# Two graph-attention layers on one core: V's products among the first scores, layer 0's sums by VectorE

## The chip, the core and the metric

The kernel runs on one core of a Trainium2 chip. A core has a matrix engine (TensorE, PE in the profile; its loads of the stationary operand are listed apart as PEld), a vector engine (VectorE, DVE), a scalar engine (ScalarE, ACT), a general one (GpSimd, POOL), and a queue that issues most DMA transfers (SyncE, SP). Each engine takes its instructions strictly in the order written and waits on semaphores for what others have to finish. Matmul results go to PSUM, which this kernel uses as four single banks of 512 columns and two pairs of banks; everything else is in SBUF. The metric is the time of the kernel on the device in microseconds; lower is better.

## What is computed

64 graphs of 256 nodes with 512 features, all in float32. Two layers, one after the other:

```python
# layer 0: one attention over the graph, scores of rank one
feat_proj = einsum('bnh,oh->bno', feats, fc_w) + fc_b
logits = q + swapaxes(k, 2, 1)             # q, k: one number per node
masked = logits + (1.0 - adj_mat) * NEG_INF
masked = where(masked >= 0, masked, 0.01 * masked)
x = einsum('bnm,bmh->bnh', softmax(masked), feat_proj) + feats
# layer 1: eight heads of 64
Q, K, V = x @ W_q + b_q, x @ W_k + b_k, x @ W_v + b_v      # by heads
scores = Q K^T / 8 + a[:, :, None] + c[:, None, :] + b_g + log(adj + 1e-9)
x = softmax(scores) V + x
```

## The kernel before, in words

Two graphs make a group: 512 nodes, 32 groups. Layer 0's weights e0 are kept transposed (neighbours on partitions). The features are mixed first (`mix`, tile `y`) and projected after, so that the projection and the three products of layer 1 are all of the form 512x512 by 512x512. Each of these is done in a Strassen-like way, with seven block products instead of eight: `pf` (layer 0's projection), `pq`, `pk`, `pv`. Their steps are called `p1` to `p7`; each is four matmul instructions of 256 columns, which stand as eight records in the trace (float32 takes two passes). `p1` starts an accumulation in a bank, `p6`, `p5` and `p3` add to it, and between them ACT copies its state out (`keep`); `p7` and `p4` share a second bank, `p2` has its own. VectorE forms the sums (`sum_00`, `sum_11`, `sum_10`; `sum_01` for `pf`) and, before the products, the sums of the moving operand's blocks (`ysum:0..3` in tile `tb`, `xsum:0..3` in tile `t1b`). p6 needs the second of these, p7 the third, p4 the fourth.

The loop is a software pipeline written out by hand (`step`, L1041, and `attention_and_layer_0`, L1000). One step works on four groups: D finishes its output, A is in layer 1's attention, F in layer 0's last part and in layer 1's products, and X, the next, is loaded and gets its layer-0 weights. The strings in these functions are lists of methods, called in that order; with `tc.manual_schedule` each engine's instructions stand in just that order.

One step's order on PE, before: scores 0 of A; `totals_1` of D (two small matmuls with `every`, which sum layer 1's weights over a graph and spread the sums over the partitions); `sums` of F (layer 0's sums as a product with a column of ones, L594); scores 1; V's `p3`, `p4` of A; `mix:0`, `mix:1`; a transpose of the layer-0 sums (`rc`, L604); `mix:2`, `mix:3`; `pf`'s p1, p2, p6, p7, p5; scores 2; `attend:0` (weights times V for graph 0 of A, tile `oT`); `totals_0`; scores 3; `pf` p3; Q's p1; `pf` p4; `attend:1`; K's p1; then Q's, K's and V's other products.

The names that matter:

- `scores:u` (L801) fills a pair of banks for each of the two neighbour tiles; ACT takes the exponent (L815), VectorE multiplies by the adjacency (`factor`, L821), and `both` adds the two tiles (L828). `parts:u` transposes that sum in 32x32 blocks and adds up its blocks' rows (L857, L858); `totals` finishes it on PE.
- `turn`, `divide`, `complete`, `store` make the output from `oTs`, the copy of `attend`'s result: a transpose (L923), a product with the reciprocal sums (L943), the residual's addition (L951) and four DMA issues on SP (L981).
- `send:o:k` transposes one block of x1 on VectorE (L729) and writes it to DRAM on SP (L733); `fetch` reads it back as four DMAs (L747), `fetch_by_both` on SP and ACT by halves. `copy:n` (L376) makes a contiguous copy of one block of x1 for V's products.
- `adjt` transposes the adjacency (L545) and makes the mask, (a - 1) * 1e9, on VectorE (L546); `add_eps` is on ACT (L550); `weights` forms e0 (L579, L583) and its exponent (L584). `dot_q`, `dot_k`, `keys` are dot products along rows on VectorE (L509); `spread` sends the result through DRAM to all partitions.
- `residual:gr` adds V's bias to x1 on ACT (L772), `turn_residual:gr` transposes it (L786).

`Mixed.keep` (L488) adds on GpSimd; that is all its work inside the loop. e0's sums, before: eight matmuls with four column positions of the array, a copy by ACT, a transpose on PE, a reciprocal on VectorE.

Of the kernel before, what the change touches and what calls it, by code (L numbers as in the profile page):

```python
# [25 lines left out]
def kernel(  # L26
# [96 lines left out]
    eps = const.tile([P, 1], F32, tag="eps", name="eps")  # L123
    nc.gpsimd.memset(eps, 1e-9)

    def column(src, tag, pool=const, q=nc.sync):
# [35 lines left out]
    def fast():  # L162
        main = ExitStack()
        with main:
# [49 lines left out]

            every = const.tile([P, HD], F32, tag="every", name="every")
            for q in range(P // B):
                for n in range(HD // B):
                    rows = slice(q * B, (q + 1) * B)
                    nc.gpsimd.tensor_copy(every[rows, ts(n, B)], ident[rows, rows])
# [167 lines left out]
            class Product:  # L387
# [3 lines left out]


                def __init__(self, name, a, b, out, rows, bias=None):
                    self.name, self.a, self.b, self.out = name, a, b, out
                    self.rows, self.bias = rows, bias
# [17 lines left out]

                def fresh(self, n):
                    dst = bank(f"{self.name}_{n}").rearrange("p (m k) -> p m k", m=2)
                    self.add(n, dst, True)
                    return dst
# [36 lines left out]
                def p7(self):  # L454
                    self.r2 = self.fresh(7)

# [49 lines left out]
            def dot_rows(src, w_row, init, dst, name):  # L506
# [5 lines left out]
                )  # L512

            class Group:

# [57 lines left out]
                def weights(self, jc):  # L573
# [10 lines left out]
                    nc.scalar.activation(e, e, AF.Exp)  # L584

                def sums(self):

                    sm = sm0.pop("bank", None)
                    begun = sm is not None
                    sm = (sm if begun else bank(f"sm0_{self.g}"))[:, 0:P]  # L590
                    for jc in range(TPG):
                        for t in range(T):
                            gr, ic = divmod(t, TPG)
                            nc.tensor.matmul(  # L594
                                sm[ts(t, RS), :], lhsT=ones[:, 0, :], rhs=self.e0[:, jc, gr, ts(ic, P)],
                                start=(jc == 0 and not begun), stop=(jc == TPG - 1),
                                tile_position=(0, t * RS), skip_group_check=True,
                            )
# [3 lines left out]
                def recip(self):  # L602
                    pt = bank(f"rc_{self.g}")[:, 0:P]
                    nc.tensor.transpose(pt, self.sms, ident)  # L604
# [29 lines left out]
                def features_first(self):  # L634

                    g = self.g
                    xT = one.tile([P, NC, TOK], F32, tag="qT", name=f"xT_{g}")
                    fp = one.tile([P, T, D], F32, tag="v", name=f"fp_{g}")
                    for t in range(T):
# [24 lines left out]
                    for t in range(T):  # L664
                        self.dot_k(t)
                    self.adjt()
                    product(1)
# [11 lines left out]
                    add_constants()  # L679
                    self.recip()  # L680
                    self.begin()
# [20 lines left out]
                def begin(self):  # L702

                    g = self.g

                    def to(dst):
                        return lambda o, k: block(dst, o, k)

                    def to_v(o, k):
                        return self.v[:, TPG * k : TPG * (k + 1), o * HALF : (o + 1) * HALF]  # L710


                    self.d = {}
# [4 lines left out]
                    self.v = one.tile([P, T, D], F32, tag="v", name=f"v_{g}")  # L718
                    b, c, self.xsum, self.copy = blocks_of_x1(self.x1T, f"t1b_{g}")
                    self.pv = Product(f"pv_{g}", "v", c, to_v, True)  # L720
                    self.pq = Product(f"pq_{g}", "q", b, to(self.qT), False, bq_col)
                    self.pk = Product(f"pk_{g}", "k", b, to(self.kT), False)

# [139 lines left out]
                def totals(self, gr, dst):  # L863
# [3 lines left out]
                    for par in range(2):  # L867
                        nc.tensor.matmul(  # L868
                            dst[par * HD : (par + 1) * HD, :].rearrange("p (a m) -> p a m", a=2),
                            lhsT=every, rhs=self.part[:, :, par * half : (par + 1) * half],  # L870
                            start=True, stop=True, skip_group_check=True,
# [3 lines left out]
                def totals_1(self):  # L875

                    sm0["bank"] = bank(f"tot_{self.g}_1")
                    self.totals(1, sm0["bank"][:, P : P + NC * N // B])

# [120 lines left out]
            def attention_and_layer_0(D, A, F, X, check):  # L1000

                A("pv.sum_11 scores:0")
                D("totals_1")
                F("sums")
                A("scores:1 pv.p3 pv.p4 factor:0:0 factor:0:1")
                D("ratios:1")
                A("both:0 factor:1:0 pv.sum_10 factor:1:1 both:1")
                check()
                F("mix:0 mix:1 ysum:0 recip")
                D("divide:1")  # L1010
                A("parts:0 residual:1")
# [12 lines left out]
                F("pk.p1 pk.keep_1")  # L1024

# [12 lines left out]

            checked, sm0 = {}, {}

            def step(d, a, f, n, check):  # L1041
# [19 lines left out]
                else:  # L1061
                    f.features_first()
                    F("pq.p1 pq.keep_1 pk.p1 pk.keep_1")
# [275 lines left out]
```

## Time and profile before

| | us |
|---|---|
| median of three runs | 2344.75 (2343.78 to 2345.67) |
| the profiled execution's own time | 2344.13 |
| its span in the profile | 2342.3 |
| ScalarE's share of the span | 42% |
| GpSimd's share | 6% |
| L801 `sc` matmuls, 2048 records, busy | 255.7 |
| L841 `oT` matmuls, 2032 records, busy | 233.4 |
| L594 `tot<-e,ones` matmuls, 480 records, busy | 19.3 |
| L604 `rc<-ident,sms` transposes, 32 records, busy | 8.7 |
| VectorE's longest wait in total: L821 for ACT's exponent | 49.6 |

All times in the profile come from one execution: its span of 2342.3 lies within its own time of 2344.13, which is 0.62 below the median of the three timed runs. The TensorE clock granted in it was 0.998 of the full one. In the groups a row reads: line, engine, operation, tile written <- tiles read, partitions x elements, count, busy time and mean duration of one. A matmul's end is modelled; its start is not. Since 16 records that follow each other overlap in the profile, the time that a group takes of PE is read from its start to the next group's start. A line of the timeline gives start and duration from the span's begin, engine, line and tiles, and in brackets the idle time before it and what ended it.

The DMA issues of one step on SP, in order: the adjacency (four), D's output (four), the four `send`s and `fetch`es of x1, the next x (one transfer of 1024 KB, which lands 5.2 us after its issue in the median, 5.0 to 8.1), A's output for graph 0 (four), and two for `spread`.

### The profile page before, as it was taken

What the parts mean: (1) busy time and instruction counts of PE and PEld (TensorE: products, weight loads), DVE (VectorE), ACT (ScalarE), POOL (GpSimd) and SP (SyncE); (2) the same over time, 40 slices, a digit from 0 to 9 for tenths busy, and PEclk for the clock granted to TensorE, in tenths of its full rate; (3) what the DMA queues carried; (4) which work ended last, traced back from release to release, by engine and by line L of the source; (5) the groups of instructions that cost most, each with busy time, mean ns of one, the idle gap of its engine ahead of it and who ended that gap; (6) DMA issues with size and microseconds to landing.
All of it is one profiled execution on the core that took longest, in us unless ns stands there. A gap on an engine that the chain in (4) does not pass through costs nothing.

```text
span 2342.3 us, 34561 instructions
## 1 busy us (share of the span) xinstructions
PE 2324.0 (99%) x13203; PEld 1907.7 (81%) x13203; DVE 2083.5 (89%) x3026; ACT 980.7 (42%) x1710; POOL 130.4 (6%) x111
## 2 busy tenths in 40 slices
PE   9999999999999999999999999999999999999997
PEld 5888888888888888888888888888888888888885
DVE  6798989889889989999899889998998989999897
ACT  3444344444444344444434444434444344444443
POOL 0000000000000000000000000000000000000000
PEclk9999999999999999999999999999999999999999
DMA  4122332223322233322233232332223332223312
GB/s 131 46 59 73 77 82 59 63 64 86 77 73 55 59 81 77 77 61 59 71 78 81 61 64 61 86 77 72 58 61 77 78 79 62 56 71 81 77 50 38
DMA packets 517267, 163.90 MB, mean 70 GB/s; under 512 B 415188, under 2 KB 478696, under 8 KB 517096
## 3 DMA queue, kind: packets, MB, share of 16 engines
q1 hardware_dynamic: 505512, 156.25, 28.9%
q10 hardware_dynamic: 11584, 5.38, 0.8%
q8 instruction: 107, 1.75, 0.3%
q14 instruction: 64, 0.52, 0.1%
HBM read 95.43 MB, written 66.12 MB: 69 GB/s over the span
## 4 chain that ended last, share of the span: by engine, by line
PE 97%; DVE 2%; DMA 1%; issue 0%; ACTq 0%; ACT 0%; DVEq 0%
PE pv L408 17%; PE pq L408 16%; PE pk L408 16%; PE pf L408 16%; PE sc L801 11%; PE y L626 9%; PE oT L841 9%; PE tot L594 1%; DMA x1T<-xd 1%; PE fp L655 1%; PE tot L868 0%; DMA xd<-xt 0%; DVE t1b L373 0%; DMA fc_nat<-in_L_gnn_fc_w_dram 0%; DVE xt L729 0%
## 5 line engine op out<-in xcount | busy, mean ns | idle before, releaser
L821 DVE TENSOR_TENSOR e<-e,am 128x1024 f32<-128x1024 f32 x254 | 303.3, 1215 | 49.7 <-ACT e L815 49.6
L815 ACT ACTIVATE e<-sc,c 128x1024 f32<-128x1024 f32 x254 | 269.2, 1111 | 42.1 <-PE sc L801 42.1
L801 PE MATMUL sc<-qT,kT 64*128 64x256 f32 x2048 | 255.7, 389 | 0.0
L488 POOL TENSOR_TENSOR pf_s<-pf_s,x 128x512 f32<-128x512 f32 x93 | 128.1, 1378 | 2130.4 <-ACT pf_s L487 2022.5
L841 PE MATMUL oT<-e,v 128*64 128x256 f32 x2032 | 233.4, 382 | 0.0
L801 PEld LDWEIGHTS sc<-qT,kT 64*128 64x128 f32 x2048 | 187.2, 186 | 46.5 <-issue 27.5
L626 PE MATMUL y<-e,x 128*128 128x256 f32 x992 | 222.6, 379 | 0.0
L841 PEld LDWEIGHTS oT<-e,v 128*64 128x64 f32 x2032 | 140.1, 137 | 85.5 <-issue 21.3
L626 PEld LDWEIGHTS y<-e,x 128*128 128x128 f32 x992 | 186.1, 190 | 26.3
L425 ACT ACTIVATE pq_s<-pq,cols 128x256 f32<-128x256 f32 x192 | 80.7, 472 | 255.3 <-PE pq L408 255.3
L487 ACT ACTIVATE pf_s<-pf,recip 128x256 f32<-128x256 f32 x186 | 78.1, 471 | 199.3 <-PE pf L408 198.1
L858 DVE TENSOR_REDUCE part<-est 128x32 f32<-128x1024 f32 x124 | 151.3, 1220 | 4.3
L857 DVE STREAM_TRANSPOSE est<-es 128x1024 f32<-128x1024 f32 x124 | 152.4, 1229 | 0.0
L848 ACT COPY oTs<-oT 128x512 f32<-128x512 f32 x128 | 75.1, 587 | 182.6 <-PE oT L841 161.7
L828 DVE TENSOR_TENSOR es<-e,e 128x1024 f32<-128x1024 f32 x126 | 148.4, 1197 | 1.2
L632 ACT COPY yT<-y 128x512 f32<-128x512 f32 x124 | 72.1, 581 | 152.4 <-PE y L626 152.4
L422 ACT COPY pk_s<-pk 128x512 f32<-128x512 f32 x96 | 56.3, 586 | 186.3 <-PE pk L408 186.3
L422 ACT COPY pv_s<-pv 128x512 f32<-128x512 f32 x96 | 55.6, 579 | 185.4 <-PE pv L408 185.4
L408 PE MATMUL pk<-x1T,wk 128*128 128x256 f32 x512 | 124.2, 385 | 0.0
L408 PE MATMUL pq<-x1T,wq 128*128 128x256 f32 x512 | 121.2, 379 | 0.2 <-DMA x1T<-xd 0.2
L408 PE MATMUL pv<-wv,t1b_c 128*128 128x256 f32 x512 | 121.1, 379 | 0.0
L408 PE MATMUL pv<-wv,t1b 128*128 128x256 f32 x512 | 121.1, 379 | 0.0
(176 smaller groups left out, 4466.9 us busy)
## 6 DMA issues: line engine op xcount, KB each, us to landing
x<-in_x_dram SPq DMA_DIRECT2D x32, 1024.0 KB, 5.2
out_dram<-osb SPq DMA_DIRECT2D x254, 128.0 KB, 3.3
xd<-xt SPq DMA_DIRECT2D x124, 256.0 KB, 2.1
x1T<-xd SPq DMA_DIRECT2D x434, 64.0 KB, 2.0
adj<-in_adj_dram SPq DMA_DIRECT2D x128, 128.0 KB, 3.8
qrow<-q SPq DMA_DIRECT2D x31, 256.0 KB, 4.1
x1T<-xd ACTq DMA_DIRECT2D x62, 64.0 KB, 2.5
fc_nat<-in_L_gnn_fc_w_dram ACTq DMA_DIRECT2D x4, 256.0 KB, 3.9
```

Of the source, the lines that this page charges most:

```text
L408: nc.tensor.matmul(o, lhsT=lk[:, ts(m, P)] if len(lk.shape) == 2 else lk[:, m], rhs=rk, start=(start and m == 0 and k == 0), stop=(m == 1 ...
L422: nc.scalar.copy(dst, src)
L425: nc.scalar.activation(dst[:, m], src[:, m], AF.Identity, bias=self.bias[:, 2 * o + m : 2 * o + m + 1],)
L488: nc.gpsimd.tensor_tensor(s, s, self.out(o, k), ALU.add)
L626: nc.tensor.matmul(y[:, ts(gr, N)], lhsT=self.x[:, gr * TPG + j, ts(c, P)], rhs=self.e0[:, j, gr, :], start=(gr == 0 and j == 0), stop=(gr ...
L801: nc.tensor.matmul(sc[:, par, pr, :], lhsT=self.kT[rows, 2 * hg + pr, ts(t, P)], rhs=self.qT[rows, 2 * hg + pr, ts(gr, N)], start=True, st ...
L815: nc.scalar.activation(e, sc, AF.Exp, bias=self.c[:, t : t + 1], scale=SCALE)
L821: nc.vector.tensor_tensor(ef, ef, self.am[:, jc, u // 2, :].unsqueeze(1).to_broadcast([P, 4, N]), ALU.mult,)
L828: nc.vector.tensor_tensor(self.esum[u], self.e[u, 0], self.e[u, 1], ALU.add)
L841: nc.tensor.matmul(oT[par * HD : (par + 1) * HD, pr, :], lhsT=self.v[:, gr * TPG + jc, ts(h, HD)], rhs=self.e[2 * gr + hg, jc][:, par, pr, :],
L857: nc.vector.transpose(turned, self.esum[u].rearrange("p a b i -> p (a b i)"))
L858: nc.vector.tensor_reduce(self.part[:, hg, :], turned.rearrange("p (m c) -> p m c", c=B), AX.X, ALU.add,)
```

## The change

On PE, `attend:1` leaves the place between `pf`'s p4 and K's p1 and goes into the next step, between scores 0 and `totals_1`, where `sums` stood; so the product with V for the second graph lies between the next step's first two scores. Scores 3 go into its former place, behind `pf`'s p4, and V's p1 goes up to just behind K's p1, ahead of Q's p6. `pq`'s p7 uses half a pair of banks instead of a single bank. V's tile becomes one tile for all groups. The order of Q's and K's products also changes (K's p6 goes between Q's p5 and p3), as does the order in which VectorE takes up factors, turns, dot products and sums; `turn`, `divide`, `complete` and `store` of the second graph are now in the next step together.

Layer 0's sums are formed by VectorE: `add_tiles` adds the two neighbour tiles, `parts_0` transposes 32x32 blocks and reduces them to 16 numbers a partition, one product with `every` (now 128 columns wide instead of 64) sums over partition blocks and spreads the result, ACT sorts it into place with four copies of 32 rows, and VectorE takes the reciprocal. The first group keeps the old way. The mask moves from one VectorE instruction to two on ACT (minus 1, times 1e9).

```diff
-            every = const.tile([P, HD], F32, tag="every", name="every")
+            every = const.tile([P, P], F32, tag="every", name="every")
...
-                def fresh(self, n):
-                    dst = bank(f"{self.name}_{n}").rearrange("p (m k) -> p m k", m=2)
+                def fresh(self, n, scores=False):
+                    name = f"{self.name}_{n}"
+                    dst = (pair(name)[:, 0] if scores else bank(name)).rearrange(
+                        "p (m k) -> p m k", m=2
+                    )
...
-                def adjt(self):
+                def adjt(self, mask=False):
...
-                    nc.vector.tensor_scalar(e0, am, 1.0, 1e9, ALU.subtract, ALU.mult)
+                    if mask:
+                        nc.vector.tensor_scalar(e0, am, 1.0, 1e9, ALU.subtract, ALU.mult)
+
+                def mask(self):
...
+                    nc.scalar.activation(e0, am, AF.Identity, bias=minus)
+                    nc.scalar.mul(e0, e0, 1e9)
...
+                def add_tiles(self):
+
+                    self.es0 = two.tile([P, TOK], F32, tag="xt", name=f"es0_{self.g}")
+                    e0, es0 = self.e0, self.es0.rearrange("p (g i) -> p g i", g=GP)
+                    nc.vector.tensor_tensor(es0, e0[:, 0], e0[:, 1], ALU.add)
+
+                def parts_0(self):
+
+                    turned = two.tile([P, TOK], F32, tag="xt", name=f"es0t_{self.g}")
+                    self.part0 = one.tile([P, TOK // B], F32, tag="part0", name=f"part0_{self.g}")
+                    nc.vector.transpose(turned, self.es0)
+                    nc.vector.tensor_reduce(
+                        self.part0, turned.rearrange("p (m c) -> p m c", c=B), AX.X, ALU.add
+                    )
+
+                def recip(self):
+
+                    pt = bank(f"rc_{self.g}")[:, 0 : TOK // B]
+                    nc.tensor.matmul(pt, lhsT=every, rhs=self.part0, start=True, stop=True)
+                    tot = one.tile([P, T], F32, tag="tot0", name=f"tot0_{self.g}")
+                    for q in range(P // B):
+                        rows = slice(q * B, (q + 1) * B)
+                        nc.scalar.copy(
+                            tot[rows, :], pt[rows, :].rearrange("p (t q) -> p q t", q=P // B)[:, q]
+                        )
+                    nc.vector.reciprocal(recip0[:, self.g, :], tot)
...
-                A("pv.sum_11 scores:0")
-                D("totals_1")
-                F("sums")
-                A("scores:1 pv.p3 pv.p4 factor:0:0 factor:0:1")
-                D("ratios:1")
-                A("both:0 factor:1:0 pv.sum_10 factor:1:1 both:1")
+                A("scores:0")
+                D("attend:1 totals_1")
+                F("add_tiles")
+                A("scores:1 factor:0:0 factor:0:1 pv.sum_11 pv.p3 pv.p4")
+                D("ratios:1 turn:1")
+                F("parts_0")
+                A("factor:1:0 factor:1:1 pv.sum_10 both:0 both:1")
                 check()
                 F("mix:0 mix:1 ysum:0 recip")
-                D("divide:1")
-                A("parts:0 residual:1")
+                D("divide:1 complete:1 store:1")
+                A("residual:1")
                 F("mix:2 mix:3 ysum:1 ysum:2 ysum:3")
-                D("complete:1 store:1")
+                A("parts:0")
                 F("pf.p1 pf.keep_1 pf.p2 pf.p6 pf.sum_00 begin send:0:0 fetch:0:0")
                 A("turn_residual:1 parts:1")
                 F("pf.p7 pf.p5")
-                A("scores:2 attend:0 totals_0 scores:3 factor:2:0 factor:2:1")
+                A("scores:2 attend:0 totals_0")
                 F("pf.sum_11 send:1:1 fetch:1:1")
-                A("ratios:0 turn:0 factor:3:0")
-                F("pf.p3 pf.sum_01 send:0:1")
-                A("factor:3:1")
-                F("pq.p1 pq.keep_1 fetch_by_both:0:1 pf.p4 pf.sum_10 send:1:0 fetch:1:0")
-                A("attend:1 both:2 both:3")
-                F("pk.p1 pk.keep_1")
+                A("factor:2:0 factor:2:1 turn:0")
+                F("pf.p3 pf.sum_01 send:0:1 pq.p1 pq.keep_1 copy:0 fetch_by_both:0:1")
+                A("ratios:0 both:2")
+                F("pf.p4 pf.sum_10 send:1:0")
+                A("scores:3")
+                F("fetch:1:0")
+                A("factor:3:0")
+                F("pk.p1 pk.keep_1 pv.p1 pv.keep_1")
...
                 F("xsum:0 xsum:1 xsum:2 pq.p6 keys:2 keys:3 keys:0 keys:1")
                 X("load_x")
+                A("factor:3:1 both:3")
+                F("pq.p7 pq.p2 pq.sum_00 xsum:3 pq.p5 pk.p6 pq.sum_11 pq.p3")
                 A("divide:0")
-                F("pq.p7 xsum:3 pq.p2 pq.sum_00")
-                A("turn:1")
-                F("pq.p5 pk.p2 pq.sum_11 copy:0 pq.p3 copy:1 copy:2 pk.sum_00")
-                A("complete:0 store:0")
-                F("pq.p4")
-                X("dot_q:0")
-                A("parts:2")
+                X("dot_q:0 dot_q:1 dot_q:2 dot_q:3 spread")
+                F("pq.p4 pq.sum_10 copy:1 copy:2")
+                A("complete:0 store:0 parts:2")
                 if n is None:
                     A("parts:3")
-                F("pq.sum_10")
-                X("dot_q:1 dot_q:2 dot_q:3 spread adjt")
-                F("pk.p6 pk.p7 pk.p5 residual:0")
+                F("pk.p7 pk.p5 pk.sum_11 residual:0")
+                X("adjt")
+                F("pk.p2 pk.sum_00")
                 X("dot_k:0 dot_k:1")
-                F("pk.sum_11")
+                F("pk.p3 pk.p4 pk.sum_10")
                 X("dot_k:2 dot_k:3")
-                F("turn_residual:0 pv.p1 pv.keep_1 pk.p3 pk.p4 pk.sum_10")
+                F("turn_residual:0")
                 if n is None:
-                    if a is not None:
-                        a.totals(1, bank("tot_last")[:, 0 : NC * N // B])
-                    A("ratios:1 divide:1 complete:1 store:1")
+                    A("attend:1 totals_1 ratios:1 turn:1 divide:1 complete:1 store:1")
...
-                X("add_eps")
+                X("mask add_eps")
                 F("pv.p2 pv.p6")
                 X("weights:0")
-                F("pv.sum_00 pv.p7 pv.p5")
+                F("pv.p7 pv.p5")
                 X("weights:1")
+                F("pv.sum_00")
                 A("parts:3")
```

More of the change, by code (lines that the diff above doesn't have):

```diff
@@ L124 @@
     nc.gpsimd.memset(eps, 1e-9)
+    minus = const.tile([P, 1], F32, tag="minus", name="minus")
+    nc.gpsimd.memset(minus, -1.0)
     def column(src, tag, pool=const, q=nc.sync):
@@ L212, in fast @@
                 nc.gpsimd.memset(ones[:, n, n : n + 1], 1.0)
-            every = const.tile([P, HD], F32, tag="every", name="every")
+            every = const.tile([P, P], F32, tag="every", name="every")
             for q in range(P // B):
-                for n in range(HD // B):
+                for n in range(P // B):
                     rows = slice(q * B, (q + 1) * B)
@@ L387, in fast @@
             class Product:
+                scores = False
                 def __init__(self, name, a, b, out, rows, bias=None):
@@ L454, in p7 @@
                 def p7(self):
-                    self.r2 = self.fresh(7)
+                    self.r2 = self.fresh(7, self.scores)
                 def p5(self):
@@ L512, in dot_rows @@
                 )
+            v_all = one.tile([P, T, D], F32, tag="v", name="v")
             class Group:
@@ L545, in adjt @@
                     nc.vector.transpose(am, self.a.rearrange("p j b c -> p (j b c)"))
-                    nc.vector.tensor_scalar(e0, am, 1.0, 1e9, ALU.subtract, ALU.mult)
+                    if mask:
+                        nc.vector.tensor_scalar(e0, am, 1.0, 1e9, ALU.subtract, ALU.mult)
+                def mask(self):
+                    flat = "p j g i -> p (j g i)"
+                    am, e0 = self.am.rearrange(flat), self.e0.rearrange(flat)
+                    nc.scalar.activation(e0, am, AF.Identity, bias=minus)
+                    nc.scalar.mul(e0, e0, 1e9)
                 def add_eps(self):
@@ L584, in weights @@
                     nc.scalar.activation(e, e, AF.Exp)
+                def add_tiles(self):
[19 more added lines that the diff above has]
+                    nc.vector.reciprocal(recip0[:, self.g, :], tot)
                 def sums(self):
-                    sm = sm0.pop("bank", None)
-                    begun = sm is not None
-                    sm = (sm if begun else bank(f"sm0_{self.g}"))[:, 0:P]
+                    sm = bank(f"sm0_{self.g}")[:, 0:P]
                     for jc in range(TPG):
@@ L595, in sums @@
                                 sm[ts(t, RS), :], lhsT=ones[:, 0, :], rhs=self.e0[:, jc, gr, ts(ic, P)],
-                                start=(jc == 0 and not begun), stop=(jc == TPG - 1),
-                                tile_position=(0, t * RS), skip_group_check=True,
+                                start=(jc == 0), stop=(jc == TPG - 1), tile_position=(0, t * RS),
                             )
@@ L600, in sums, with recip_of_sums @@
                     nc.scalar.copy(self.sms, sm)
-                def recip(self):
+                def recip_of_sums(self):
                     pt = bank(f"rc_{self.g}")[:, 0:P]
@@ L637, in features_first @@
                     xT = one.tile([P, NC, TOK], F32, tag="qT", name=f"xT_{g}")
-                    fp = one.tile([P, T, D], F32, tag="v", name=f"fp_{g}")
+                    fp = v_all
                     for t in range(T):
@@ L665, in features_first @@
                         self.dot_k(t)
-                    self.adjt()
+                    self.adjt(True)
                     product(1)
@@ L679, in features_first @@
                     add_constants()
-                    self.recip()
+                    self.recip_of_sums()
                     self.begin()
@@ L717, in begin @@
                     self.kT = one.tile([P, NC, TOK], F32, tag="kT", name=f"kT_{g}")
-                    self.v = one.tile([P, T, D], F32, tag="v", name=f"v_{g}")
+                    self.v = v_all
                     b, c, self.xsum, self.copy = blocks_of_x1(self.x1T, f"t1b_{g}")
@@ L721, in begin @@
                     self.pq = Product(f"pq_{g}", "q", b, to(self.qT), False, bq_col)
+                    self.pq.scores = True
                     self.pk = Product(f"pk_{g}", "k", b, to(self.kT), False)
@@ L869, in totals @@
                             dst[par * HD : (par + 1) * HD, :].rearrange("p (a m) -> p a m", a=2),
-                            lhsT=every, rhs=self.part[:, :, par * half : (par + 1) * half],
+                            lhsT=every[:, 0:HD], rhs=self.part[:, :, par * half : (par + 1) * half],
                             start=True, stop=True, skip_group_check=True,
@@ L875, in totals_1 @@
                 def totals_1(self):
-                    sm0["bank"] = bank(f"tot_{self.g}_1")
-                    self.totals(1, sm0["bank"][:, P : P + NC * N // B])
+                    self.totals(1, bank(f"tot_{self.g}_1")[:, 0 : NC * N // B])
                 def totals_0(self):
@@ L1037, in check_ranges @@
                 return flag_ready
-            checked, sm0 = {}, {}
+            checked = {}
             def step(d, a, f, n, check):
@@ L1062, in step @@
                     f.features_first()
[L1063 removed]
+                    F("pq.p1 pq.keep_1 copy:0 pk.p1 pk.keep_1 pv.p1 pv.keep_1")
                 F("xsum:0 xsum:1 xsum:2 pq.p6 keys:2 keys:3 keys:0 keys:1")
                 X("load_x")
+                A("factor:3:1 both:3")
+                F("pq.p7 pq.p2 pq.sum_00 xsum:3 pq.p5 pk.p6 pq.sum_11 pq.p3")
                 A("divide:0")
[L1067 to L1073 removed]
+                X("dot_q:0 dot_q:1 dot_q:2 dot_q:3 spread")
+                F("pq.p4 pq.sum_10 copy:1 copy:2")
+                A("complete:0 store:0 parts:2")
                 if n is None:
                     A("parts:3")
[L1076 to L1078 removed]
+                F("pk.p7 pk.p5 pk.sum_11 residual:0")
+                X("adjt")
+                F("pk.p2 pk.sum_00")
                 X("dot_k:0 dot_k:1")
[L1080 removed]
+                F("pk.p3 pk.p4 pk.sum_10")
                 X("dot_k:2 dot_k:3")
[L1082 removed]
+                F("turn_residual:0")
                 if n is None:
[L1084 to L1086 removed]
+                    A("attend:1 totals_1 ratios:1 turn:1 divide:1 complete:1 store:1")
                     F("residual:1 turn_residual:1")
```

## The prediction, before the result was known

> **What bounds the kernel now.** I read the page's busy row and chain first.
>
> ```profile
> PE 2324.0 (99%) x13203; PEld 1907.7 (81%) x13203; DVE 2083.5 (89%) x3026; ACT 980.7 (42%) x1710; POOL 130.4 (6%) x111
> ...
> PE 97%; DVE 2%; DMA 1%; issue 0%; ACTq 0%; ACT 0%; DVEq 0%
> ```
>
> TensorE (PE) is busy for 99% of the span and carries 97% of the chain. Matmul ends are modelled, so I checked with starts alone: the timeline of PE over one middle step (start, busy, line, tiles, count; stretches left out).
>
> ```profile
> 1083.30 2.00 PE L801 MATMUL sc<-qT,kT 64*128 64x256 f32 x16
> 1085.22 0.31 PE L868 MATMUL tot<-part,every 128*64 128x32 f32 x4
> 1085.46 0.64 PE L594 MATMUL tot<-e,ones 128*32 128x128 f32 x16
> 1086.04 2.00 PE L801 MATMUL sc<-qT,kT 64*128 64x256 f32 x16
> ...
> 1094.98 0.27 PE L604 MATMUL rc<-ident,sms 128*128 128x128 f32 x1
> 1095.09 3.62 PE L626 MATMUL y<-e,x 128*128 128x256 f32 x16
> ...
> 1109.19 3.67 PE L841 MATMUL oT<-e,v 128*64 128x256 f32 x32
> 1112.70 0.26 PE L868 MATMUL tot<-part,every 128*64 128x32 f32 x4
> 1112.89 2.00 PE L801 MATMUL sc<-qT,kT 64*128 64x256 f32 x16
> ...
> 1118.37 1.89 PE L408 MATMUL pf<-fcT,tb 128*128 128x256 f32 x8
> 1120.19 3.67 PE L841 MATMUL oT<-e,v 128*64 128x256 f32 x32
> 1123.80 1.99 PE L408 MATMUL pk<-x1T,wk 128*128 128x256 f32 x8
> 1125.64 3.69 PE L408 MATMUL pq<-t1b,q_s 128*128 128x256 f32 x16
> 1129.17 1.89 PE L408 MATMUL pq<-x1T,wq 128*128 128x256 f32 x8
> 1130.89 1.89 PE L408 MATMUL pq<-t1b,wq 128*128 128x256 f32 x8
> ```
>
> See that a product of 8 records takes 1.727 us from its start to the next start (1129.17 to 1130.89; three decimals here and below are medians of the same difference over 29 steps of the trace): 0.216 us a record, step after step, so PE runs without pauses. A change of tile shape costs about 0.1 us on each side (1.82 for the `pf` product before `oT`). From one step's first scores to the next, the starts give a median of 71.86 us and a mean of 71.96. So the end is a sum of PE starts, 31 steps of it, and other engines count only where PE waits for them. The view of PE's waits has one that recurs:
>
> ```profile
> PE pq L408 <- DVE t1b L373: 2.2, 5, 0.9
> ```
>
> That is p6 of Q waiting for the sums of x1. Part of it is not booked as waiting: `pq` from 1125.64 to 1129.17 is 3.53 for 16 records, where 3.45 is normal, and `pk` before it 1.84 where 1.83 is normal after a shape change. So a usual step loses 0.09 there, and the mean shows 0.08 to 0.10 more, from some six steps in which a transfer of x1 is late.
>
> **The change on PE, part by part.**
> - The 16 `ones` records of layer 0's sums go: 1085.46 to 1086.04 is 0.574 us. 31 steps: -17.8.
> - `totals_1` no longer runs into them but into scores, as `totals_0` does now (0.187 in place of 0.238): 30 x 0.05 = -1.5.
> - `attend:1` stands between scores 0 and `totals_1`. Entered from `pf` it takes 3.604 (1120.19 to 1123.80), entered from scores 3.505 (1109.19 to 1112.70): 30 x 0.10 = -3.0.
> - The recurring loss before Q's p6 goes: V's p1 (1.727) and scores 3 take the place of `attend:1` as cover. 31 x 0.09 = -2.8; whether the cover holds is worked out below. The late transfers stay.
> - The transpose `rc` (0.109 to the next start) becomes a product of `every`, 128 columns of weights, with 16 moving columns, two records. No row is the same. Low end: the transpose's 0.11. High end 0.4: two of its weight loads and the next product's, none hidden, by the 0.13 between the two starts of the one-column product at L285 (9.64 and 9.77). I take 0.22, two passes at about that pace: 31 x 0.11 = +3.4.
> - `totals_0` is followed by `pf` instead of scores: between nothing and 0.1 for the shape, 0.05 taken: +1.6.
> - The first step's wait before Q's p6 (2.88 from pk's start in place of 1.84) is covered once: -1.
>
> Sum: -17.8 - 1.5 - 3.0 - 2.8 + 3.4 + 1.6 - 1.0 = **-21.1 us**.
>
> Here the Trainium skill can be weighed. "TensorE: Matmul & The Clock Gate", section "Back-to-back issue gap", gives 81 ns a matmul in a sustained stream at 128 columns; its sum for the 16 records would be 1.3 us a step and a gain of 40 us. The row, 0.036 us each (four 32-column strips share the array), decides: 17.8. A second rule speaks against the change: "Perfetto Trace Analysis", section "Identifying the Most-Contended Engine", says not to judge TensorE by matmul busy time but by weight loads, and to call the engine with the highest occupancy the bound. Here that is 81% against VectorE's 89%: VectorE would be the bound, and its 1.3 us of added work a step (next part) would cost 31 x 1.3 = +41. The row is against it: the starts stand 0.216 us apart whatever VectorE does. I follow the row, and keep the rule as the slower rival.
>
> **The other engines: does the cover hold?** I laid one new step out by hand, in the changed instruction order, each engine's durations from its rows, time 0 at the first scores. PE, with the terms above: attend:1 1.93, totals 5.43, scores 1 5.62, V's p3 7.55, y 11.11, recip 14.56, pf1 18.2, pf2 20.0, scores 2 27.0, attend:0 28.9, pf3 32.6, pq1 34.5, pf4 36.2, scores 3 38.0, pk1 39.9, pv1 41.8, pq6 43.5, pq2 47.0, pk4 62.5, pv2 64.2, next step 71.2.
> - VectorE gets an add (128x512, 0.69), a transpose (0.71) and a reduction (half of the 1.22 for 1024 columns, 0.61) and loses a TENSOR_SCALAR (0.69): +1.32. It gets back about 1.08: `complete:1` stands beside GpSimd's add now and takes 2.29 instead of 1.21 in half its cases; in the new order it starts near 17.3, GpSimd near 21. The step has 71.2, its work is some 65.5, and in my layout it still waits for PE or ACT nine times, 5 us in all, so a lag dies out within a step.
> - ACT gets two passes over 128x1024 (the row for `am` is 1.15 each) and four 32-row copies (at most the 0.27 of `sms` each), and loses `sms`: +3.1 on 31.9 of 75. The copies stand before `xv` and the copy of y2, which comes at 18.2; pf2 needs it at 20.0. The two passes lie at 63.1 to 65.2, behind `adjt` (62.0) and ahead of V's keep (67.7); the weights need them at 67.7.
> - Queued behind totals_1 is all of PE; the partial sums it needs are done at 3.3 for 5.43. The bank of attend:1's second half is freed by V's sum at about 0.9 for 3.7; y2's bank at 12.4 for 14.8; the layer-0 partial sums at 9.5 for 14.56.
> - SP: the store of `complete:1` starts at 18.4, so its four issues (2.97) are done before `send:0:0` at 24.9 (now the send waits for them: 1107.11 and 1107.20). The next x is issued at 46.4 and lands 5.2 later (8.1 at most); dot_q:0, now earlier, asks at 53.1. The adjacency load waits for the last partial sums, 3.3, and is due at 60.8.
> - The tightest place is Q's p6. pf3 ends at 34.5, VectorE's x and transpose follow as now (transpose starts 1.12 later, 35.6). In the row the transpose starts at 1117.76, the reload at 1120.67, two issues and 2.5 of landing end it 5.85 after: 41.4. ACT issues half of it, so the exponent of scores 3 waits behind that until about 39; its factor now stands ahead of the sums: 40.3 to 41.5. From the first sum to p6 the row has 1.56 (1124.08 to 1125.64): **43.04 for 43.50**. So 0.46 spare, where now there is none.
> - Next: K's sums free banks for pk4 (60.8 for 62.5) and pv2 (62.7 for 64.2).
>
> These hide the rest; where a cover is gone, 1 us late in each step is 31 us. At the start GpSimd makes eight more copies of `every` (8 of them take 1.54 us at L219) and is then idle for 66.7 us until its first add. In the closing section the last `attend:1` and `turn:1` stand among K's last sums: the same PE records, and about 0.5 us more on VectorE ahead of the last group's first factors, where it later idles 1.88 us before a sum of V.
>
> **Time.** The profiled execution took 2344.13 (span 2342.3 and 1.8 around it); minus 21.1 gives 2323.0. The median is 0.6 above it: **2323.6**.
>
> **Rivals.**
> - The cover fails at p6: the row's transfer varies, and exponent, factor and sums are in one file. The 0.09 stays and a late case is added in one step of three, 0.15 a step: 31 x 0.15 more = 2328. For it: six late steps now. Against: 0.46 spare. Chance 0.14.
> - VectorE comes late at K's sums: it fills the 1.5 and PE waits 0.5 a step: 2339. For it: 92% load and no PE wait to absorb a lag between 51 and 62. Against: VectorE waits just before, at 51.3. Chance 0.07.
> - PE's small parts are cheaper: recip hidden (-3.4), no price after totals (-1.6), half the late transfers gone (-1.5): 2317. Chance 0.06.
> - Slower: VectorE is the bound at one place, the stretch from dot_q:0 to K's sums. Up to a lag of 1.6 at pk4 nothing happens; each us beyond costs PE one us, the change's 0.68 a step is used up at 2.3, and at a lag of 3 the time is 2344.75 + 31 x (1.4 - 0.68) = 2367. For it: the rule above, and x landing late there. Against: even a landing of 8.1 makes a lag of only 1.4. Chance 0.03.
>
> **Range and chances.** Forecast 0.70. The PE terms' own ends, recip 0 to 0.3 and totals 0 to 0.1, give -5 to +7; with the first and third rival, 2315 to 2333. About 0.2%, 4.7 us, is what can be told from no change. Faster 0.94, within 0.03, slower 0.03.
>
> **What would show it.** The profile after should have `sc` 1.93, `oT` 3.50, `tot` 0.19, `sc`; a `rc` of 0.2 between the `y`; `pq` at 3.45 for 16 records; a step of 71.2; `osb<-osb,xb` at 1.2 throughout. A PE wait on `kT`, or `pq` still at 3.53 or above, would prove the cover wrong; VectorE without waits would prove the rule right.

## The result, and the profile after

Four runs of the changed kernel took 2324.06 us in the median (2323.66 to 2326.03); the kernel before took 2344.40 in four (2343.78 to 2345.67). The ratio is 0.9914, with a 95% interval of 0.9897 to 0.9931. The forecast was 2323.6 in a range of 2315 to 2333. The profiled execution took 2324.43, its span 2322.6, at a granted clock of 0.998 as before.

The busy row on the page of the kernel after:

```profile
PE 2302.7 (99%) x12738; PEld 1906.0 (82%) x12738; DVE 2092.7 (90%) x3088; ACT 1071.0 (46%) x1865; POOL 122.0 (5%) x120
```

PE has 465 records fewer (13203 to 12738) and is still busy for 99% of the span (and carries 95% of the chain on the same page): the time is still a sum of PE starts. Where it went is read from PE's timeline over one step's beginning (start, busy, line, tiles, count), to be laid beside the one of before:

```profile
1142.94 2.00 PE L843 MATMUL sc<-qT,kT 64*128 64x256 f32 x16
1144.87 3.67 PE L883 MATMUL oT<-e,v 128*64 128x256 f32 x32
1148.37 0.26 PE L910 MATMUL tot<-part,every 128*64 128x32 f32 x4
1148.56 2.00 PE L843 MATMUL sc<-qT,kT 64*128 64x256 f32 x16
1150.49 1.99 PE L412 MATMUL pv<-v_s,t1b_c 128*128 128x256 f32 x8
1152.32 1.89 PE L412 MATMUL pv<-wv,t1b 128*128 128x256 f32 x8
1154.05 3.62 PE L667 MATMUL y<-e,x 128*128 128x256 f32 x16
1157.50 0.29 PE L621 MATMUL rc<-part,every 128*128 128x16 f32 x2
1157.64 3.70 PE L667 MATMUL y<-e,x 128*128 128x256 f32 x16
```

The `ones` group between `tot` and `sc` is gone and `oT` has its place; scores 1 start 0.19 after `tot`, and `rc` takes 0.14 to the next start where the transpose took 0.11. The step, from first scores to first scores, has a median of 71.16 us (before 71.86) and a mean of 71.33 over 29 steps (before 71.96). The tightest place of the prediction, Q's p6, in an ordinary step (same view):

```profile
1111.66 1.99 PE L412 MATMUL pk<-x1T,wk 128*128 128x256 f32 x8
1113.49 1.89 PE L412 MATMUL pv<-wv,t1b_c 128*128 128x256 f32 x8
1115.22 3.62 PE L412 MATMUL pq<-t1b,q_s 128*128 128x256 f32 x16
1118.67 1.89 PE L412 MATMUL pq<-x1T,wq 128*128 128x256 f32 x8
```

`pq` lasts 3.45 for its 16 records where it lasted 3.53: it no longer waits. VectorE's first sum of x1 starts at 1113.24 there, and p6 wants its data 1.56 later, at 1114.80: 0.42 us to spare. In six of the 29 steps it still comes late. One line of PE's waits (engine, tile, line, releaser; total, times, longest) and the timeline of the longest case, with the same lines of an ordinary step below it:

```profile
PE pq L412 <- DVE t1b L375: 3.3, 6, 1.3
```

```profile
323.12 0.34 SPq L775 DMA_DIRECT2D xd<-xt  x1
...
327.09 0.78 SPq L789 DMA_DIRECT2D x1T<-xd  x2
...
1108.04 0.34 SPq L775 DMA_DIRECT2D xd<-xt  x1
...
1110.06 0.78 SPq L789 DMA_DIRECT2D x1T<-xd  x2
...
1113.24 0.69 DVE L375 TENSOR_TENSOR t1b<-x1T 128x512 f32<-128x512 f32 x1
```

The reload (L789) can be issued only when the write (L775) has landed: 3.97 us after its issue in the late step, 2.02 in the ordinary one. So p6 came 1.5 us late. In two of the six it is the write that lands late, in four the reload.

### The profile page after: what moved, and what is told of

The parts are those of the page before. It is cut to its first block, busy times and chain, and to the rows that moved or that the text cites. A ratio compares the mean times of both kernels' runs of the same rounds, so it can differ in the third digit from the quotient of the medians.

```text
span 2322.6 us, 33706 instructions
## 1 busy us (share of the span) xinstructions
PE 2302.7 (99%) x12738; PEld 1906.0 (82%) x12738; DVE 2092.7 (90%) x3088; ACT 1071.0 (46%) x1865; POOL 122.0 (5%) x120
## 4 chain that ended last, share of the span: by engine, by line
PE 95%; DVE 2%; DMA 2%; issue 0%; ACT 0%; ACTq 0%; DVEq 0%
PE pv L412 17%; PE pq L412 16%; PE pk L412 16%; PE pf L412 16%; PE sc L843 10%; PE oT L883 10%; PE y L667 9%; DMA x1T<-xd 1%; DMA xd<-xt 1%; PE fp L696 1%; DVE t1b L375 0%; DMA fc_nat<-in_L_gnn_fc_w_dram 0%; PE tot L910 0%; DVE xt L771 0%; PE rc L621 0%
## 5 line engine op out<-in xcount | busy, mean ns | idle before, releaser
L495 POOL TENSOR_TENSOR pf_s<-pf_s,x 128x512 f32<-128x512 f32 x93 | 118.5, 1274 | 2118.7 <-ACT pf_s L494 1673.4
L412 PE MATMUL pk<-t1b,wk 128*128 128x256 f32 x512 | 121.1, 379 | 0.4 <-DVE kT L443 0.4
```

The costliest lines, as they stand in the source:

```text
L412: nc.tensor.matmul(o, lhsT=lk[:, ts(m, P)] if len(lk.shape) == 2 else lk[:, m], rhs=rk, start=(start and m == 0 and k == 0), stop=(m == 1 ...
L495: nc.gpsimd.tensor_tensor(s, s, self.out(o, k), ALU.add)
```

## The experiments

The theory: the time is a sum of PE starts, 0.7 us a step shorter, and all the other work added lies in cover. The rivals: VectorE is the bound somewhere; or the two parts of the change (sums on VectorE, the V product between the scores) do not add up as booked.

**1. The new order alone** (e1). The kernel after, with layer 0's sums put back on PE:

```diff
-                F("add_tiles")
+                F("sums")
...
-                F("parts_0")
...
-                F("mix:0 mix:1 ysum:0 recip")
+                F("mix:0 mix:1 ysum:0 recip_of_sums")
```

`totals_1` runs into the sums' bank again, as before.

> The changed kernel with layer 0's sums back on TensorE as before (ones products, transpose); all moves of attend:1, V's p1 and the mask stay. Theory (TensorE's starts add up, VectorE is covered): a step gets the 0.574 of the ones products and 0.05 of totals back and loses 0.224 for 0.109 at the reciprocal, 71.16 + 0.51 = 71.67 in the median; 31 x 0.51 = 16 us, so about 2340 us. Rival (VectorE's load counts, here 1.9 us a step less): the late waits shrink too and the time stays under 2332.

Measured: 2341.24 (2339.25 to 2342.78, 20 runs) beside 2343.73 for the kernel before, ratio 0.9987 (0.9980 to 0.9994); median step 71.62. That is against the rival (under 2332). The order alone brings 0.24 us in the usual step, but only 0.11 in the mean (71.85 for 71.96), since the late steps cost more. The median lies 0.05 under the 71.67 expected. The timeline of PE, behind `attend:1`, shows why:

```profile
1085.01 0.26 PE L913 MATMUL tot<-part,every 128*64 128x32 f32 x4
1085.20 0.64 PE L638 MATMUL tot<-e,ones 128*32 128x128 f32 x16
```

`totals_1` runs into the `ones` records again and takes 0.187 all the same; it does not go back to 0.238.

**2. The sums alone** (e2). The kernel before, with only the sums moved to VectorE:

```diff
-                F("sums")
+                F("add_tiles")
...
+                F("parts_0")
```

> The kernel before with layer 0's sums alone moved to VectorE (add, transpose, reduction, one product with the wide tile, four copies); order of attention and products and the mask as before. Theory: a step loses 0.574 and 0.05 and gains 0.115, 71.86 - 0.51 = 71.35 in the median, about 2329 us, and keeps the 0.09 before Q's p6 (16 pq records in 3.53). Rival (VectorE, 67 of 71 us a step without the earlier complete:1, is too full): the sums come late somewhere, a new wait of PE for VectorE appears and the time is 2335 or more.

Measured: 2340.83 (2339.75 to 2342.75, 20 runs), ratio 0.9987 (0.9980 to 0.9994); median step 71.72, where 71.35 was expected. The sums' records are gone from PE, and the step is only 0.14 shorter. The number is on the rival's side, but by another way than the rival's: PE does not wait for VectorE. The timeline of PE and ACT at that place in this kernel:

```profile
1083.25 2.00 PE L825 MATMUL sc<-qT,kT 64*128 64x256 f32 x16
...
1084.43 2.12 ACT L839 ACTIVATE e<-sc,c 128x1024 f32<-128x1024 f32 x2
1085.18 0.31 PE L892 MATMUL tot<-part,every 128*64 128x32 f32 x4
...
1085.60 2.14 PE L825 MATMUL sc<-qT,kT 64*128 64x256 f32 x16
1086.78 2.12 ACT L839 ACTIVATE e<-sc,c 128x1024 f32<-128x1024 f32 x2 [0.23 <-PE sc L825]
1087.67 1.99 PE L408 MATMUL pv<-v_s,t1b_c 128*128 128x256 f32 x8
```

Scores 0 and scores 1 use the same two pairs of banks. ACT takes the exponent of scores 0 from the first pair between 1084.43 and about 1085.5, and PE's next scores want that pair at 1085.42, 0.24 after `tot`; they start at 1085.60. From `tot` to `sc` it is 0.421 in the median, where the same totals behind scores took 0.238 before, and `sc` takes 2.069 where 1.927 is normal, since its second pair is late too: 0.325 lost. With the 0.574 gone and 0.115 more for `rc`, the step is 0.134 shorter, as measured. PE's own list of waits has 0.4 once. The wait stands with the weight loads, which come before the matmuls (view of PEld's waits):

```profile
PEld sc L825 <- ACT e L839: 15.9, 62, 0.8
```

This is twice a step, 0.5 us a step of idle loads. In the kernel before, the 0.574 us of `ones` records covered this time.

**3. Another cover for the exponent** (e8). If that reading holds, any PE work between the two scores must bring the loss back. The kernel of experiment 2, with V's p3 moved there:

```diff
-                A("pv.sum_11 scores:0")
+                A("pv.sum_11 scores:0 pv.p3")
...
-                A("scores:1 pv.p3 pv.p4 factor:0:0 factor:0:1")
+                A("scores:1 pv.p4 factor:0:0 factor:0:1")
```

> The kernel before with layer 0's sums by VectorE, as in the run with the sums alone, and V's p3 moved up between scores 0 and totals_1. New theory (what took the gain there is ACT's exponent: scores 1 need the two pairs of banks of scores 0, and the ones products had been filling just that time): with 1.83 us of other work between, scores 1 take 1.93 and totals 0.19 again; two more changes of shape cost 0.2; median step 71.72 - 0.38 + 0.2 = 71.54. Rival (VectorE's fuller load is what delays): scores 1 and totals stay at 2.07 and 0.42 and the step at 71.9.

Measured: 2335.76 (one run; before beside it 2343.77), median step 71.60. Scores 1 take 1.927 again and no weight load waits for the exponent. The totals (PE's timeline) do not come back to the 0.19 expected:

```profile
1084.43 0.31 PE L892 MATMUL tot<-part,every 128*64 128x32 f32 x4
1084.67 2.00 PE L825 MATMUL sc<-qT,kT 64*128 64x256 f32 x16
```

They take 0.239 behind V's p3, although they run into scores. So the 0.325 of experiment 2 is back. p3 pays for two more changes of shape (1.924 for its eight records instead of 1.83, and 0.10 more for p4 behind the scores), so 0.12 of it remains as gain.

**4. V's p1 back in its old place** (e3). The kernel after, with the cover of Q's p6 halved:

```diff
-                F("pk.p1 pk.keep_1 pv.p1 pv.keep_1")
+                F("pk.p1 pk.keep_1")
...
-                F("turn_residual:0")
+                F("turn_residual:0 pv.p1 pv.keep_1")
...
```

> The changed kernel with V's p1 back behind the last residual transpose, as before; the rest as changed. Theory (the reload of x1 sets the earliest start of Q's p6, and the 1.73 us of V's p1 are what covers it, 0.42 to spare): p6 waits 1.31 us, and 0.09 for the start from a standstill, in every usual step: 71.16 + 1.40 = 72.56, about 2324 + 43 = 2367 us. Rival (the transfer is hidden anyway, place of V's p1 is free): 71.2 a step, 2324 us.

Measured: 2370.07 (one run), median step 72.57. PE's waits:

```profile
PE pq L412 <- DVE t1b L375: 40.6, 31, 2.7
```

Every one of 31 steps now waits there. V's p1 is worth 1.73 us of cover, of which 0.42 was to spare, so 1.31 is waited for, with 0.09 for the start from a standstill, as expected.

**5. More work for VectorE** (e4, e5). The kernel after, with two and with four more dot products of 0.73 us each behind the present four; their results go to a spare tile.

```diff
-                X("dot_q:0 dot_q:1 dot_q:2 dot_q:3 spread")
+                X("dot_q:0 dot_q:1 dot_q:2 dot_q:3 spread extra:0 extra:1")
```

> The changed kernel with two more dot products (1.46 us) on VectorE behind the four of the next x, written to a spare tile. Theory (K's sums free their banks 1.59 us ahead of need for pk's p4): covered, median step 71.16 to 71.25, about 2324 to 2327 us. Rival (VectorE's load sets the end): 1.46 us a step more, 2369 us.

> The changed kernel with four more dot products (2.92 us) at the same place. Theory: 1.59 are covered, PE waits 1.33 and about 0.09 for the standing start at pk's p4 in each of 30 steps: median step 72.6, about 2367 us. Rival (VectorE's load sets the end): 2.92 a step, 2414 us; rival (VectorE never counts): 2324 us.

Measured with two (1.46 us a step): 2329.01, median step 71.20. With four (2.92): 2374.51, median step 72.67; one run each. The page's busy row with two, and PE's waits with four:

```profile
PE 2307.3 (99%) x12738; PEld 1904.7 (82%) x12738; DVE 2135.2 (92%) x3212; ACT 1073.0 (46%) x1865; POOL 124.3 (5%) x120
```

```profile
PE pk L413 <- DVE kT L444: 37.8, 31, 1.5
```

VectorE at 92% instead of 90% costs the median step 0.04. From two products to four, 1.46 us more work makes it 1.46 longer, and this is waited for where the prediction put the place, at K's sums before p4; 1.41 of the 2.92 is covered (the step grew by 1.51).

Both times lie above what was expected (2324 to 2327, and about 2367). A part lies ahead of the first scores, which start 1.5 us later in these runs than in the run after. Another part stood in neither the prediction's layout nor the expectation: every fourth step VectorE also checks the reciprocal sums' range (`ok`, L1030 to L1037 of the kernel after), in six small instructions that take 1.6 us together. VectorE's timeline with two products, in such a step, whose first scores start at 930.94:

```profile
946.44 0.17 DVE L1036 TENSOR_SCALAR ok<-recip 128x16 f32<-128x16 f32 x1
...
957.31 0.71 DVE L777 STREAM_TRANSPOSE xt<-x 128x512 f32<-128x512 f32 x1
```

The step's first `send` starts 26.4 us after the scores, where it starts at 24.2 in the other steps. In the kernel after, VectorE idles 1.3 us ahead of it in the other steps and not at all in these, and the send starts at 24.3 at most; there the check just fits. With two products the lag reaches Q's p6 in all seven of these steps, which are 0.3 to 0.8 us longer than the median, 3.4 us in all (0.4 of it at K's p4, in one of them). In the kernel after none of the seven is late. So the dot products do cost there; the other five late steps are late in the kernel after too, by their transfers.

**6. The mask back on VectorE** (e9).

```diff
-                X("adjt")
+                X("adjt:1")
...
-                X("mask add_eps")
+                X("add_eps")
```

> The changed kernel with the mask back on VectorE (one instruction, 0.61 us more there behind adjt; two passes less on ACT). Theory (1.59 us to spare at K's sums): covered, median step 71.16. Rival (VectorE's load sets the end): 0.61 a step, 71.8.

Measured: 2325.36 (one run), median step 71.16. No gain or loss from that part of the change can be seen here; the mask lay in cover on either engine.

**7. More cover for the transfers** (e6, then e7). The late steps are what is left over, so the transfers should start earlier. First try, on the kernel after: `pf`'s p3 and p4, whose output is transposed, written and reloaded, go in front of `attend:0`.

```diff
-                A("scores:2 attend:0 totals_0")
-                F("pf.sum_11 send:1:1 fetch:1:1")
...
+                A("scores:2")
+                F("pf.sum_11 send:1:1 fetch:1:1 pf.p3 pf.sum_01 send:0:1")
+                F("pf.p4 pf.sum_10 send:1:0 fetch_by_both:0:1")
+                A("factor:2:0 factor:2:1 attend:0 totals_0")
+                F("pq.p1 pq.keep_1 copy:0 fetch:1:0")
+                A("turn:0 ratios:0 both:2 scores:3")
```

> The changed kernel with pf's p3 and p4 right behind scores 2, then attend:0 and totals_0, Q's p1, scores 3, K's and V's p1; x1's last two blocks are sent some 3.5 us earlier against Q's p6, and its sums stand ahead of the factor of scores 3. Theory (what is left of waiting is late reloads of x1, 0.17 us a step in the mean, 1.3 at most): they vanish in the larger cover, mean step 71.2 instead of 71.33, about 2319 us. Rival (the tighter places in front of it, the bank for pf's p4 and the partial sums, now wait): a new wait of PE for VectorE at pf or tot and 2324 us or more.

Measured: 2335.51 (2334.69 to 2337.07, 5 runs), ratio 0.9964 (0.9950 to 0.9978): slower than the kernel after by some 11 us, and the expectation was wrong. Nor is the rival's wait there: PE does not wait at `pf` or `tot`. The timeline of one of the late steps, queues SP and ACT and VectorE's wait:

```profile
1110.23 1.73 SPq L789 DMA_DIRECT2D x1T<-xd  x4
...
1112.06 0.85 SPq L775 DMA_DIRECT2D xd<-xt  x2
...
1114.24 0.82 ACTq L789 DMA_DIRECT2D x1T<-xd  x2
...
1115.16 1.07 ACT L890 COPY oTs<-oT 128x512 f32<-128x512 f32 x2 [8.53 <-PE pq L412]
...
1116.27 1.25 DVE L963 STREAM_TRANSPOSE osb<-oTs 128x1024 f32<-128x1024 f32 x1 [3.00 <-ACT oTs L890]
```

Two queues stood still. On SP the write of the next block came behind four reloads, which waited for the block before. ACT's half of the reload waited for that write until 1114.24, and ACT's copies of `oT`, though `oT` was done by 1112.41, stood behind it (the bracket names `pq`, but they start when ACT's two issues end, 1114.24 + 0.82); so VectorE idled 3.00 us for them. In the usual step the cover hardly grew (about 2.1 us from first sum to p6, for 1.96), and twelve of 29 steps came late (mean 71.62). The median's 0.20 (71.36) are two more changes of shape on PE: Q's p1, between totals and scores, takes 1.924 for 1.727.

Second try (e7): the write goes ahead of the reloads, all reloads are on SP, and scores 3 stand right behind `totals_0`, so that no shape change is added.

```diff
-                A("scores:2 attend:0 totals_0")
-                F("pf.sum_11 send:1:1 fetch:1:1")
-                A("factor:2:0 factor:2:1 turn:0")
-                F("pf.p3 pf.sum_01 send:0:1 pq.p1 pq.keep_1 copy:0 fetch_by_both:0:1")
-                A("ratios:0 both:2")
-                F("pf.p4 pf.sum_10 send:1:0")
-                A("scores:3")
-                F("fetch:1:0")
+                A("scores:2")
+                F("pf.sum_11 send:1:1 pf.p3 pf.sum_01 send:0:1 fetch:1:1")
+                F("pf.p4 pf.sum_10 send:1:0 fetch:0:1")
+                A("factor:2:0 factor:2:1 attend:0 totals_0 scores:3")
+                F("pq.p1 pq.keep_1 copy:0 fetch:1:0")
+                A("turn:0 ratios:0 both:2")
+                F("pk.p1 pk.keep_1 pv.p1 pv.keep_1 xsum:0 xsum:1 xsum:2")
                 A("factor:3:0")
-                F("pk.p1 pk.keep_1 pv.p1 pv.keep_1")
...
```

> A second try at more cover for Q's p6: as the run with attend:0 late, but scores 3 right behind totals_0 (two changes of shape less), x1's third block sent ahead of the second's reload, and all reloads issued by SyncE, so that ACT doesn't stand behind one. Theory (there, ACT's copies waited for the reload's issue and VectorE for ACT, and two shape changes cost 0.2): median step 71.16 and no late steps but the largest, mean 71.2, about 2320 us. Rival (the places in front are too tight also so): median above 71.3, 2326 us or more.

Measured: 2320.74 (2320.18 to 2322.09, 4 runs) beside 2343.77 for the kernel before, ratio 0.9902 (0.9886 to 0.9919). It is 23.0 below the kernel before that ran beside it; the kernel after was 20.3 below its own. The two did not run side by side and their intervals overlap, but their runs do not (2322.09 at most, 2323.66 at least). Its timeline, PE and VectorE:

```profile
1109.83 0.69 DVE L375 TENSOR_TENSOR t1b<-x1T 128x512 f32<-128x512 f32 x1 [0.23 <-DMA x1T<-xd]
...
1113.54 3.62 PE L412 MATMUL pq<-t1b,q_s 128*128 128x256 f32 x16
```

From first sum to p6 there are 3.71 us in this step (2.55 to 4.08 in all), where 1.56 are needed; the spare is 2.15 instead of 0.42. Writes still land up to 4.0 us after their issue, but within the cover. All 29 steps last 71.16 us, and the line `pq <- t1b` is gone from PE's waits.

## Why the prediction was right, point by point

The path, PE's starts, was right, and so was nearly every size; one size was right for a wrong reason. Each step of the sum, with what the trace after and the runs showed:

| step of the sum | predicted, us a step | measured |
|---|---|---|
| `ones` records gone | -0.574 | -0.574, but only with `attend:1` in their place: 30 steps, not 31 |
| `totals_1` into scores | -0.05 | -0.05 (0.187 for 0.238), but for what stands ahead of it |
| `attend:1` entered from scores | -0.10 | -0.10 (3.504) |
| usual loss before Q's p6 | -0.09 | -0.09 (`pq` 3.453) |
| product `rc` for the transpose | +0.11 | +0.115 (0.140 to the next start, and 0.084 more for the `y` behind it) |
| `totals_0` before `pf` | +0.05 | 0 (0.188) |
| late transfers (mean minus median step) | 0 | +0.07 (0.17 for 0.10) |

The predicted gain of 21.1 stands against 19.7 between the two spans (2342.3 and 2322.6). Of the 1.4 us that are missing, the late transfers make 2.0, `totals_0` gives 1.6 back, the first step loses 0.57 that was booked (below), and `rc` 0.15; about 0.3 stays untraced. The first step's single wait went as said: 2.88 before Q's p6 became 1.73 behind a product without a shape change, 1.0 saved.

**The term for `totals_1`** was lucky. It supposed that the totals get cheaper because they run into scores instead of the `ones` records. Experiment 1 lets them run into the `ones` records and they take 0.187; experiment 3 lets them run into scores and they take 0.239. What differs is the work ahead: `attend`, whose tile shape in the rows is that of the totals (128*64), or scores and V's p3, which have another. So the 0.05 belongs to the move of `attend:1`. `totals_0`, the example the prediction took, also stood behind `attend:0`.

**The step that was right by less than it claimed** is the first. It priced the `ones` records at their length, as if work that leaves a full PE always frees its time. Median steps of four kernels show otherwise:

| | sums on PE | sums on VectorE |
|---|---|---|
| nothing new between scores 0 and 1 | 71.86 (before) | 71.72 (e2) |
| `attend:1` between them | 71.62 (e1) | 71.16 (after) |

The sums are worth 0.46 in the lower row (0.574 less the 0.115 of the product, and next to nothing else) and 0.14 in the upper one. The layout followed the scores' banks only for `attend:1` and V's sum and took for granted that ACT had emptied scores 0's pairs when scores 1 began; with `attend:1`, 3.5 us between them, it had. The kernel after shows it itself, in its first step, which has no earlier graph and so no `attend:1` (PE's timeline):

```profile
75.45 2.00 PE L843 MATMUL sc<-qT,kT 64*128 64x256 f32 x16
77.80 2.14 PE L843 MATMUL sc<-qT,kT 64*128 64x256 f32 x16 [0.35 <-ACT e L857]
79.87 1.99 PE L412 MATMUL pv<-v_s,t1b_c 128*128 128x256 f32 x8
```

From the first scores to V's product it is 4.42 us there, and it was 4.43 before (75.56 to 79.99), with the `ones` records between: they went and nothing was gained. The total came out since both parts were in the change. A forecast for the sums alone would have missed by some 12 us, as the expectation for experiment 2 did (2329 for 2340.83). The prediction's terms for the order alone (`attend:1`, Q's p6, `totals_0`, first step) come to 5.2 us; experiment 1 measured 2.5.

**The late transfers** were to stay as they were. Their cost grew by 0.07 us a step, about 2 us, which is inside the range; that is the mild form of the first rival (0.15 a step, 2328). Experiment 7 shows that it is these transfers, by covering them. Mean minus median is 0.10 before and 0.11 with the sums alone, but 0.23 with the order alone: in these profiles, one of each, it comes with the new order and not with VectorE's sums. Why, the runs do not show.

**The covers** held as laid out: 0.42 at Q's p6 (0.46 predicted), 1.59 at K's p4 (kT's sum ends at 1132.62, p4 starts at 1134.21; 1.6 was the lag predicted to be free, and experiment 5 gives 1.41). Experiment 4 shows what the first costs when gone, experiment 5 the second. The layout was of a usual step and left out the range check; that a lag of VectorE "dies out within a step" held for the change and failed with 1.46 us more, in every fourth step. `complete:1` came back to 1.2 us in all its cases (22 of its 31 took 2.29 before, where the prediction said half); its groups before and after, one line of each kernel (times of one: least, median, longest in ns):

```profile
L951 DVE TENSOR_TENSOR osb<-osb,xb x62: 1211/1215/2295, 128.2 to 2302.4; 128x1024 f32<-128x1024 f32 x62
```

```profile
L991 DVE TENSOR_TENSOR osb<-osb,xb x62: 1211/1220/1227, 129.0 to 2284.0; 128x1024 f32<-128x1024 f32 x62
```

**The slower rival** stood on the rule of the Trainium skill, "Perfetto Trace Analysis", section "Identifying the Most-Contended Engine", by which VectorE's 89% beside 81% of weight loads would make it the bound. (The page judges TensorE also by its share of the peak rate, which is not worked out here.) Experiment 5 is the test: VectorE's share rose from 90% to 92% and the median step by 0.04. A share does not say where the slack lies; in the usual step the slack was 1.4 to 1.6 us in one place, and beyond it the rule's engine did decide, at 1 us for 1 us. In the steps with the range check it was used up earlier.

## What to carry to other kernels

Work that leaves the bounding engine frees its time only if nothing else was using that time as cover: look for who empties the buffer that the next instruction fills, and when, before you book its length. Price a change of two parts for each part alone as well; where the parts do not add up, one covers for the other. Lay out the steps that do more than the usual one as well: the cover of the usual step is not theirs. And where a few steps in thirty are late, compare the mean of the step with its median: what stands between them is bought back by starting the transfer earlier, as long as no queue that the new order uses stands waiting in front of other work.

## What the runs showed of the hardware

- A matmul that waits for a buffer may show no idle PE: in experiment 2 the 0.325 us a step is in longer groups (`tot` 0.421 for 0.238, `sc` 2.069 for 1.927), and only the weight loads' list books the wait (15.9 us, 62 times, where PE's has 0.4).
- Four records of the totals cost 0.187 us behind records of the same tile shape (128*64) and 0.238 behind others (scores, V's p3), whatever followed them.
- A product of two records with 16 moving columns costs 0.140 to the next start, and 0.084 more in the group behind it (3.537 for the usual 3.453): 0.224 in all.
- Late transfers of x1 come in certain steps. Counted from the first step with scores as 0, Q's p6 waits for them in steps 2, 3, 10, 17, 18 and 25 of the kernel after, in five of these with two more dot products, and in 2, 10, 17 and 25 with the mask on VectorE; most lie 7 or 8 steps apart. In the kernel before it is in 13, 17, 21, 25 and 29, each one step behind a range check. No run tests whether the check has to do with it; the cause stays open.
- VectorE's addition of two tiles took up to 2.295 us beside GpSimd's additions and never more than 1.227 when the order kept them apart.
